# Keys and queries of a chunk by seven block products in place of eight

## The chip, the cores and the metric

The kernel runs on one core of one Trainium2 chip. The metric is the device time of one execution in microseconds (us). Smaller is better. All tensors are float32.

## The reference, cut to what matters

Two layers are computed on four images of 512 channels and 64x64 pixels. The first layer is self-attention over the 4096 pixels of an image, with 128 channels for queries, keys and values. The second layer is an involution: a 7x7 filter whose 49 weights are made for every pixel. Both add their input back.

```python
# layer 0, for each of 4 images; xf has 512 channels and 4096 pixels
q = wq @ xf + bq            # 128 x 4096
k = wk @ xf + bk            # 128 x 4096
v = wv @ xf + bv            # 128 x 4096
attn = softmax(q.T @ k)     # 4096 x 4096
x = wo @ (v @ attn.T) + bo + x
# layer 1
o = relu(s1 * (W1 @ x) + b1)                   # 128 channels
w = Ws @ relu(sr * (Wr @ o) + br) + bs         # 49 weights for each of 8 groups and each pixel
y = sum over the 49 taps of w[tap] * o shifted by the tap
out = s3 * (W3 @ y) + b3 + x
```

## The kernel before, in words

One image is handled after the other (variable b). A chunk is 512 pixels of an image, eight to an image (variable c). A chunk of x is a tile of 128 partitions by 4 blocks of channels by 512 pixels.

**The key stage** (keys_values) of an image goes over its chunks in the order 2, 3, 4, 5, 6, 7, 1, 0. For each chunk TensorE makes the keys pk (four products of a 128x128 weight block with 512 pixels, accumulated over the channels) and the values pv (sixteen products with 128 columns). ScalarE copies both out of PSUM and adds the key bias. Each product of float32 shows as two instructions in the profile.

**The attention stage** (attention) goes over blocks of 512 queries. At each of 32 steps a block of 128 keys is scored against the queries (pss), ScalarE takes the exponential (pt), TensorE accumulates the values (po), and VectorE sums the exponentials (pacc). The queries of a block (pq, four products with 512 columns, made by queries) are computed eight steps before the block begins. Those of chunk 0 are made in the key stage.

**The end of a block** (finish_block) divides by the sums, multiplies by wo (pwo), adds the residue, multiplies by W1 (p1), and writes the result with a border to DRAM (pix), from which windows of rows are read back (ring).

**The involution** runs beside all this. For two rows of pixels at a time TensorE makes the weights (pw), VectorE multiplies them with the ring (prod, line 427) and GpSimd adds the products up (acc, line 447). Such a multiplication with its addition is called a tap here. Then the sum is turned (turned), multiplied by W3 (py), added to x, and stored.

**What sets the order.** The program keeps an account of its own time: every matmul adds its columns times 0.43/256 us to a variable pe, and takes adds the cost of an operation to the account of VectorE or GpSimd. chores is called between matmuls; it lets the end of a block, the close of an involution unit, and the taps take a step. A tap waits while VectorE is more than 3.5 us ahead of pe in the account (4.5 in the last image) or GpSimd more than lag (4.0 in the key stage, 7.5 in attention). What is not done when attention ends is done in a tail, in which TensorE shares the additions.

**Buffers.** The exponentials lie in five tiles of the pool pt, scores in two PSUM banks (s), po and pacc in one bank each, the general products in two (mm). x has six tiles. All loads and stores of this part go through SyncE's one queue in the order of the program.

The lines that the change and the prediction touch: load_x at 215, keys_values at 589, queries at 626, attention at 779, the main loop at 837, and the wait of a tap at 392.

Of the kernel before, what the change touches and what calls it, by code (L numbers as in the profile page):

```python
# [8 lines left out]
F32 = mybir.dt.float32  # L9
# [6 lines left out]
P = 128  # L16
# [52 lines left out]

PE_COLUMN = 0.43 / 256  # L70
DVE_OP, POOL_OP = 0.7, 1.28
DVE_TAPS, POOL_TAPS = (0.16, 0.27), (0.19, 0.55)
ROW_US, X_US, PIX_US, LAND_US = 2.2, 3.8, 1.5, 3.0
HOP_US = 0.8
# [15 lines left out]
def fast_path(  # L90
# [22 lines left out]
    def pool(name, bufs, **kw):  # L113
# [37 lines left out]
    okr = const.tile([P, 1], F32, name="okr")  # L151


    turns = [
        scratch.tile([CH // P, P, P], F32, tag=f"turns{i}", name=f"turns{i}") for i in range(2)
    ]
# [14 lines left out]
    reds, sums_c = {}, {}  # L171
    written = {}
    landing = {}
    lag = 0.0
    low, load = 0, 0

    def until(us):
# [40 lines left out]
        nc.sync.dma_start(xs[b, c], x_r[b, :, :, c * CH : (c + 1) * CH])  # L218


    for cols in (slice(0, P), slice(P, O_WV)):
        nc.scalar.dma_start(wt[:, cols], wts[:, cols])
    nc.scalar.dma_start(vec, vecs)
    c0, c1 = KEYS[:2]
    xs = {(0, c0): xpool.tile([P, CT, CH], F32, tag="x", name=f"x_0_{c0}")}
    for t in range(CT):
        nc.sync.dma_start(xs[0, c0][:, t, :], x_r[0, :, t, c0 * CH : (c0 + 1) * CH])
    nc.sync.dma_start(wt[:, O_WV:O_WQ], wts[:, O_WV:O_WQ])
    load_x(0, c1)
    nc.sync.dma_start(wt[:, O_WQ:], wts[:, O_WQ:O_WR])  # L230
    nc.vector.memset(ones, 1.0)

    warm = ps.tile([P, P], F32, tag="mm", name="warm")
# [13 lines left out]
    def w_slice(off, t):  # L247
        return wt[:, off + t * P : off + (t + 1) * P]
# [4 lines left out]
    def mm(o, lhsT, rhs, start=True, stop=True, shared=1):  # L253
        pe_us(rhs.free_size() * PE_COLUMN / shared)
        return nc.tensor.matmul(o, lhsT=lhsT, rhs=rhs, start=start, stop=stop)  # L255
# [52 lines left out]
    def chores():  # L308
        step(finishing, 1)
        step(closing, 1)  # L310
        pace()
# [40 lines left out]
    def involution():  # L352
        nonlocal low, due
        while True:
# [24 lines left out]
            for o, (tiles, x, dy, n) in enumerate(ops):  # L379
                if ending:  # L380
                    sums = parts[tiles[0]]
                if o and dy >= DYS[1][0] > ops[o - 1][2]:
                    low = base + UR
                    pump()
                    if tail and units:
                        early[units[0]] = weights(*units[0])
                        copies[units[0]] = copied(*units[0], early[units[0]])
                rows = [(base + dy + t * 2) % RING for t in range(NT)]
                while base + dy + n + 2 * tiles[-1] > load:
                    yield "wait"  # L390
                landed = max(landing[base + dy + 2 * t + i] for t in tiles for i in range(n))
                while not tail and (
                    pe < max(begin, landed)
                    or free["dve"] > pe + (4.5 if b == B - 1 else 3.5)
                    or free["pool"] > pe + lag
                ):
                    yield "wait"
                first = x == 0 and dy < DYS[1][0]
                maker = adder = None
                if tail:  # L400
                    if pw_copy is None:
                        pw_copy = copies.pop((b, u), None) or copied(b, u, pw)
                    maker, adder = share(
                        n * len(tiles) * P, not first, first or ending and o >= len(ops) - 6
                    )
                cost = n * len(tiles) / NT
                free["pool"] = max(free["pool"], takes("dve", DVE_TAPS[0] + DVE_TAPS[1] * cost))
                takes("pool", POOL_TAPS[0] + POOL_TAPS[1] * cost)
                due -= cost
                d0 = dy - DYS[dy >= DYS[1][0]][0]  # L410
                prod, p0 = acc, d0
                if not first:
                    home = tailpools[1] if maker == "dve" else prods
                    prod, p0 = home.tile(
                        [P, NT, 4, P], F32, tag="prod", name=f"prod_{b}_{u}_{o}"
                    ), 0
                nt, these = len(tiles), slice(tiles[0], tiles[-1] + 1)
                col = (x * K + dy) * G
                row = rows[tiles[0]]
                lines = ring[:, row : row + n, x, :]  # L420
                image = bass.AP(
                    tensor=lines.tensor, offset=lines.offset,
                    ap=[lines.ap[0], [(rows[1] - rows[0]) * K * P, nt], [K * P, n], [1, P]],
                )
                made = prod[:, these if first else slice(0, nt), p0 : p0 + n, :]
                maps = pw_copy if maker == "pool" else pw
                product = (nc.gpsimd if maker == "pool" else nc.vector).tensor_tensor(  # L427
                    made.rearrange("p t d (g c) -> p t d g c", g=G),
                    image.rearrange("p t d (g c) -> p t d g c", g=G),
                    maps[:, these, col : col + n * G].unsqueeze(3)  # L430
                    .broadcast_to([P, nt, n * G, GC])
                    .rearrange("p t (d g) c -> p t d g c", d=n),
                    ALU.mult,
                )
                if not tail:
                    tc.keep_in_program_order(product)
                if first:
                    pass
                elif adder == "pe":

                    closes = ending and o == len(ops) - 1
                    if ending and o == len(ops) - 3:
                        drain(sums)
                        add_sums(sums["pa"], acc, False, tiles)
                    adds.append((spent[maker], o + 100 * u, sums, prod, tiles, n, closes))
                else:
                    nc.gpsimd.tensor_tensor(  # L447
                        acc[:, these, d0 : d0 + n, :], acc[:, these, d0 : d0 + n, :],
                        prod[:, :nt, :n, :], ALU.add,
                    )  # L450
                if tail:
                    drain()
                if ending and (o == len(ops) - 1 or ops[o + 1][0] != tiles):
                    closing.append(turn_last(b, u, tiles, acc, sums))
                yield
# [130 lines left out]
            nc.sync.dma_start(out_r[b, :, :, c * CH + off : c * CH + off + n], xt)  # L586


    def keys_values(b):
        kt = kvpool.tile([P, N], F32, tag="k", name=f"k_{b}")  # L590
        vT = kvpool.tile([P, N // P, P], F32, tag="v", name=f"v_{b}")

        for i, c in enumerate(KEYS):
            for k in KEYS[i + 1 : i + 3]:
                if (b, k) not in xs:
                    load_x(b, k)
            if c == 0:

                q = queries(b, 0, 0, CH)
            if b < 2 and i == 4:  # L600
                for rows in (slice(0, PAD), slice(PAD + H, None)):
                    nc.sync.dma_start(pix[b][rows].rearrange("r w c -> w r c"), zero)
                for cols in (slice(0, PAD), slice(PAD + W, None)):
                    nc.sync.dma_start(pix[b][PAD : PAD + H, cols, :], zero[:H])
            xt = xs[b, c] if c < KEEP else xs.pop((b, c))
            pk = ps_s.tile([P, CH], F32, tag="s", name=f"pk_{b}_{c}")
            for t in range(CT):
                mm(pk, w_slice(O_WK, t), xt[:, t, :], t == 0, t == CT - 1)
                if t % 2:
                    chores()  # L610
            nc.scalar.activation(
                kt[:, c * CH : (c + 1) * CH], pk, AF.Identity, bias=v1(V_BK)
            )
            pv = ps1.tile([P, 4, P], F32, tag=("po", "acc")[i % 2], name=f"pv_{b}_{c}")
            for j in range(4):
                for t in range(CT):
                    mm(
                        pv[:, j, :], xt[:, t, j * P : (j + 1) * P], w_slice(O_WV, t),
                        t == 0, t == CT - 1,
                    )  # L620
                if j % 2:
                    chores()
            nc.scalar.copy(vT[:, 4 * c : 4 * c + 4, :], pv)
        return kt, vT, q

    def queries(b, c, off, n):
        xt = xs[b, c][:, :, off : off + n]
        pq = ps.tile([P, CH], F32, tag="mm", name=f"pq_{b}_{c}_{off}")[:, :n]
        for t in range(CT):
            mm(pq, w_slice(O_WQ, t), xt[:, t, :], t == 0, t == CT - 1)  # L630
        q = work2.tile([P, CH], F32, tag="q", name=f"q_{b}_{c}_{off}")[:, :n]
        nc.scalar.activation(q, pq, AF.Identity, bias=v1(V_BQ))
        return q


# [200 lines left out]

    taps = [involution()]
    for b in range(B):
        lag = POOL_LAG[0]
        kv = keys_values(b)  # L840
        lag = POOL_LAG[1]
        if b == 0:

            pb = ps.tile([P, CT], F32, tag="mm", name="pb")
# [435 lines left out]
```

## Time and profile before

| what | value |
|---|---|
| median of 3 runs | 2587.23 us (2586.75 to 2587.34) |
| the profiled execution | 2587.14 us |
| its span in the profile | 2585.2 us, so 1.9 us lie around it |
| TensorE busy | 2570.4 us |
| VectorE busy | 1862.6 us |
| GpSimd busy | 1825.2 us |
| ScalarE busy | 838.2 us |
| granted clock of TensorE | 0.999 |
| DMA | 243 MB, 38.9% of 16 engines' span in SyncE's queue |

The profile page lists busy time by engine, the span in 40 slices, the DMA queues, and the chain of work that ended last, followed back from the last instruction. Groups of instructions can be asked for by line and shape, with the mean duration of one. Records of consecutive matmuls overlap, so the distance between starts in the chain, not the mean duration, says what a matmul costs in a row.

The key stages of the four images lie at 5 to 65, 616 to 690, 1249 to 1322 and 1878 to 1955 us, and the last score of the last image ends at about 2530 us. What follows is the tail.

### The profile page before, as it was taken

The numbers are of one execution on the slowest core, as the hardware profiler recorded it, in microseconds if no ns is written. First come the engines' busy times: TensorE is split into PE (matmuls) and PEld (weight loads), VectorE is DVE, ScalarE is ACT, GpSimd is POOL, SyncE is SP. The second block draws the span as 40 slices with busy tenths as digits, with TensorE's granted clock in tenths as the row PEclk, the third lists the DMA queues.
The fourth block names the chain that finished last, engine by engine and source line by source line (L and its number), as shares of the span: only waits on it lengthen the run. The fifth ranks groups of instructions, "written<-read, shape, count | busy, mean of one in ns | idle before, by whom it ended". The sixth has DMA issues, their size and how long they took to land.

```text
span 2585.2 us, 24342 instructions
## 1 busy us (share of the span) xinstructions
PE 2570.4 (99%) x7367; PEld 1229.3 (48%) x7367; DVE 1862.6 (72%) x2678; ACT 838.2 (32%) x1386; POOL 1825.2 (71%) x1207
## 2 busy tenths in 40 slices
PE   9999999999999999999999999999999999999998
PEld 7444444445544444444554444444465444444476
DVE  0347778887585777888667667878857678787888
ACT  1333333332233333333223333333322333333331
POOL 0006788877881778888786368888788567887887
PEclk9999999999999999999999999999999999999999
DMA  6033233445615343234661434433364431332343
GB/s 238 1 74 62 58 77 83 98 102 148 151 60 114 64 102 69 68 81 99 166 153 41 108 69 96 102 70 92 79 181 112 110 90 47 90 78 61 78 95 101
DMA packets 209049, 243.36 MB, mean 94 GB/s; under 512 B 109640, under 2 KB 129040, under 8 KB 208784
## 3 DMA queue, kind: packets, MB, share of 16 engines
q1 hardware_dynamic: 208480, 241.39, 38.9%
q8 instruction: 59, 0.97, 0.2%
q14 instruction: 78, 0.64, 0.1%
q10 hardware_dynamic: 432, 0.36, 0.1%
HBM read 192.65 MB, written 49.06 MB: 93 GB/s over the span
## 4 chain that ended last, share of the span: by engine, by line
PE 92%; POOL 4%; DVE 3%; issue 1%; ACT 0%; DVEq 0%; POOLq 0%
PE pss L255 32%; PE po L255 31%; PE pv L255 4%; PE pk L255 4%; PE pq L255 4%; PE p L255 4%; PE pwo L255 4%; PE py L255 4%; POOL acc L447 4%; PE pw L255 2%; DVE prod L427 1%; DVE pacc L828 1%; PE pr L255 1%; PE pa L259 1%; POOL acc L462 0%
## 5 line engine op out<-in xcount | busy, mean ns | idle before, releaser
L447 POOL TENSOR_TENSOR acc<-acc,prod 128x768 f32<-128x768 f32 (+3 forms) x1052 | 1682.8, 1617 | 737.9 <-DVE prod L427 694.6
L255 PE MATMUL pss<-q,k 128*128 128x512 f32 (+1 forms) x2112 | 1055.7, 584 | 0.0
L255 PE MATMUL po<-pt,v 128*128 128x512 f32 (+1 forms) x2112 | 1047.3, 580 | 0.0
L797 ACT ACTIVATE pt<-pss 128x512 f32<-128x512 f32 x1024 | 611.1, 597 | 1242.6 <-PE pss L255 1188.8
L427 DVE TENSOR_TENSOR prod<-ring,pw 128x768 f32<-128x768 f32 (+3 forms) x1086 | 874.7, 840 | 46.0 <-POOL acc L447 44.9
L828 DVE TENSOR_TENSOR pacc<-pacc,pt 128x512 f32<-128x512 f32 x958 | 664.8, 694 | 237.9 <-ACT pt L797 209.9
L255 PEld LDWEIGHTS po<-pt,v 128*128 128x128 f32 x2112 | 398.8, 190 | 480.9 <-issue 460.4
L255 PEld LDWEIGHTS pss<-q,k 128*128 128x128 f32 x2112 | 391.4, 190 | 466.8 <-issue 462.0
L508 DVE STREAM_TRANSPOSE turned<-acc 128x256 f32<-128x256 f32 x48 | 21.4, 445 | 217.9 <-POOL acc L462 217.9
L255 PE MATMUL py<-accT,wt 128*128 128x512 f32 (+1 forms) x256 | 130.1, 590 | 4.5 <-DVE x L577 4.5
L255 PE MATMUL pwo<-on,wt 128*128 128x512 f32 (+1 forms) x264 | 128.6, 580 | 0.1
L462 POOL TENSOR_TENSOR acc<-acc 128x512 f32<-128x512 f32 x122 | 121.4, 995 | 9.6
L255 PEld LDWEIGHTS pv<-wt,x 128*128 128x128 f32 x1024 | 119.6, 192 | 15.3 <-issue 15.1
L577 DVE SCALAR_TENSOR_TENSOR x<-py,vec,x 128x512 f32<-128x512 f32 (+2 forms) x136 | 96.4, 711 | 36.2 <-PE py L255 35.7
L255 PE MATMUL pv<-wt,x 128*128 128x128 f32 x1024 | 120.2, 275 | 0.0
L255 PE MATMUL p<-x,wt 128*128 128x512 f32 (+1 forms) x264 | 119.3, 580 | 0.0
L255 PE MATMUL pk<-x,wt 128*128 128x512 f32 x256 | 117.1, 596 | 0.0
L706 ACT ACTIVATE x<-x,vec 128x512 f32<-128x512 f32 (+1 forms) x132 | 92.9, 706 | 74.2 <-PE p L255 58.1
L255 PE MATMUL pq<-x,wt 128*128 128x512 f32 (+1 forms) x264 | 115.3, 579 | 0.0
L679 DVE SCALAR_TENSOR_TENSOR x<-pwo,bo,x 128x512 f32<-128x512 f32 (+1 forms) x132 | 95.1, 727 | 21.3 <-PE pwo L255 19.9
L427 DVE TENSOR_TENSOR acc<-ring,pw 128x1024 f32<-128x1024 f32 (+1 forms) x85 | 78.7, 945 | 15.6 <-PE pw L255 15.6
L255 PEld LDWEIGHTS pq<-x,wt 128*128 128x128 f32 x264 | 50.1, 190 | 59.7 <-issue 56.4
(74 smaller groups left out, 727.0 us busy)
## 6 DMA issues: line engine op xcount, KB each, us to landing
x<-x_dram SPq DMA_DIRECT2D x55, 1024.0 KB, 5.7
ring<-pix SPq DMA_DIRECT2D x74, 448.0 KB, 7.0
ring<-pix SPq DMA_DIRECT2D x24, 1344.0 KB, 9.7
out_dram<-x SPq DMA_DIRECT2D x31, 1024.0 KB, 4.5
ring<-pix SPq DMA_DIRECT2D x24, 896.0 KB, 10.5
ring<-pix SPq DMA_DIRECT2D x30, 672.0 KB, 10.9
ring<-pix SPq DMA_DIRECT2D x6, 2240.0 KB, 19.5
pix<-o1t SPq DMA_DIRECT2D x192, 32.0 KB, 1.7
```

The lines of the kernel that those rows point to most:

```text
L255: return nc.tensor.matmul(o, lhsT=lhsT, rhs=rhs, start=start, stop=stop)
L259: nc.tensor.matmul(o, lhsT=lhsT, rhs=ident, start=start, stop=stop, is_transpose=True)
L427: product = (nc.gpsimd if maker == "pool" else nc.vector).tensor_tensor(made.rearrange("p t d (g c) -> p t d g c", g=G), image.rearrange(" ...
L447: nc.gpsimd.tensor_tensor(acc[:, these, d0 : d0 + n, :], acc[:, these, d0 : d0 + n, :], prod[:, :nt, :n, :], ALU.add,)
L462: nc.gpsimd.tensor_tensor(acc[:, :, :n, :], acc[:, :, :n, :], acc[:, :, n : 2 * n, :], ALU.add)
L508: nc.vector.transpose(blocks.rearrange("p (t k q) -> p t k q", t=NT, q=TB), acc[:, :, 0, :].rearrange("p t (k q) -> p t k q", q=TB),)
L577: nc.vector.scalar_tensor_tensor(xt[:, t, :], py, v1(V_S3 + t), xt[:, t, :], ALU.mult, ALU.add)
L679: nc.vector.scalar_tensor_tensor(xt[:, t, :], pw, bo[:, t : t + 1], xt[:, t, :], ALU.add, ALU.add)
L706: nc.scalar.activation(xt[:, t, :], xt[:, t, :], AF.Identity, bias=v1(V_B3 + t))
L797: nc.scalar.activation(pt, pss, AF.Exp)
L828: nc.vector.tensor_tensor(paccs[k], paccs[k], pt, ALU.add)
```

## The change

The weights of keys and queries are stacked to 256 rows by 512 channels, and cut into two by two blocks; a chunk of x is cut into two by two blocks of 256 channels by 256 pixels. Their product is formed by Strassen's scheme in Winograd's form: seven products of blocks (m1 to m7) in place of eight, each of two matmuls with 256 columns. So a chunk's keys and queries are made together in the key stage.

- Sums of the weights (s1, s2, s4, and a difference put in place of the first half of wq) are made once, by VectorE, in the first chunk.
- Four differences of blocks of x (pixel_sums, 128x512 each) are made per chunk: for an image's first chunk two on VectorE and two on GpSimd, else all four on GpSimd, one chunk ahead, in tiles of the pool pt.
- ScalarE copies m1; VectorE makes seven additions of 128x256 from PSUM, four of them with a bias.
- Queries of chunks 1 to 7 are written to DRAM (q_out) and read back by queries, where before they were computed. Queries of chunk 0 stay in SBUF.
- The values of a chunk are split: twelve of sixteen matmuls after the fourth product, the last four after the seventh. Their PSUM tile is always po; before it alternated with acc, which now holds m5 and m3. m1 and m2 share a bank of s, m6 and m7 the other.
- In the key stage a tap waits while VectorE is 2.5 us ahead (before 3.5 or 4.5) or GpSimd 2.5 (before 4.0).
- At the start the weights of values are loaded first, those of keys and queries next, the others later.

```diff
+HALF_OP = 0.4
+KEY_LAG = 2.5
...
-                    or free["dve"] > pe + (4.5 if b == B - 1 else 3.5)
+                    or free["dve"] > pe + (2.5 if making else 4.5 if b == B - 1 else 3.5)
...
+    def pixel_sums(b, c, ahead):
+        (b11, b12), (b21, b22) = halves(b, c)
+        out = []
+        for n, (x0, x1) in enumerate(((b12, b11), (b22, 0), (b22, b12), (b21, 1))):
+            pt = ptpool.tile([P, CH], F32, tag="pt", name=f"sum_{b}_{c}_{n}")
+            pt = pt.rearrange("p (t n) -> p t n", t=2)
+            slow = ahead or n > 1
+            takes("pool" if slow else "dve", POOL_OP if slow else DVE_OP)
+            (nc.gpsimd if slow else nc.vector).tensor_tensor(
+                pt, x0, out[x1] if x1 in (0, 1) else x1, ALU.subtract
+            )
+            out.append(pt)
+        return out
...
+        def product(o, w, rhs):
+            for t in range(2):
+                mm(o, w[:, t * P : (t + 1) * P], rhs[:, t, :], t == 0, t == 1)
...
+                    nc.vector.tensor_tensor(s1, q10, q1, ALU.add)
+                    nc.vector.tensor_tensor(s2, s1, k0, ALU.subtract)
+                    nc.vector.tensor_tensor(s4, k1, s2, ALU.subtract)
+                    nc.vector.tensor_tensor(q10, k0, q10, ALU.subtract)
...
+            def add(o, m, with_, bias=None):
+                takes("dve", HALF_OP)
+                if bias is None:
+                    nc.vector.tensor_tensor(o, m, with_, ALU.add)
+                else:
+                    nc.vector.scalar_tensor_tensor(o, m, v1(bias), with_, ALU.add, ALU.add)
+
+            product(m1, k0, b11)
+            nc.scalar.copy(left, m1)
+            product(m6, s2, t2)
+            product(m7, q10, t3)
+            add(right, m6, left)
+            add(q[:, :HF], m7, right)
+            product(m5, s1, t1)
+            add(q[:, HF:], m5, q[:, :HF], V_BQ)
+            add(right, m5, right)
+            if i + 1 < NCH:
+                sums = pixel_sums(b, KEYS[i + 1], True)
...
+            product(m2, k1, b21)
+            add(left, m2, left, V_BK)
+            product(m6, q1, t4)
+            add(q[:, :HF], m6, q[:, :HF], V_BQ)
+            product(m3, s4, b22)
+            add(right, m3, right, V_BK)
+            if c:
+                nc.sync.dma_start(q_out[c], q)
...
     def queries(b, c, off, n):
-        xt = xs[b, c][:, :, off : off + n]
-        pq = ps.tile([P, CH], F32, tag="mm", name=f"pq_{b}_{c}_{off}")[:, :n]
-        for t in range(CT):
-            mm(pq, w_slice(O_WQ, t), xt[:, t, :], t == 0, t == CT - 1)
         q = work2.tile([P, CH], F32, tag="q", name=f"q_{b}_{c}_{off}")[:, :n]
-        nc.scalar.activation(q, pq, AF.Identity, bias=v1(V_BQ))
+        nc.sync.dma_start(q, q_out[c][:, off : off + n])
         return q
...
-        lag = POOL_LAG[0]
+        lag, making = KEY_LAG, True
         kv = keys_values(b)
-        lag = POOL_LAG[1]
+        lag, making = POOL_LAG[1], False
```

## The prediction

> **What bounds the kernel now.** I read the page's busy row and its chain of waits first.
>
> ```profile
> PE 2570.4 (99%) x7367; PEld 1229.3 (48%) x7367; DVE 1862.6 (72%) x2678; ACT 838.2 (32%) x1386; POOL 1825.2 (71%) x1207
> ...
> PE 92%; POOL 4%; DVE 3%; issue 1%; ACT 0%; DVEq 0%; POOLq 0%
> ```
>
> TensorE is busy for 99% of the span and is 92% of the chain. The rest of the chain (POOL 4%, DVE 3%) lies mostly in the tail. So a matmul column taken away is worth its time, as long as nobody makes TensorE wait. Next the busy time by stretches (columns: length, then busy us of PE, PEld, DVE, ACT, POOL, clock, DMA share, GB/s): the key stage of image 1, a stretch of image 3's attention, and the tail.
>
> ```profile
> 616.00:690.00 74.00, 74.00 (x370) 48.12 (x369) 38.10 (x45) 15.48 (x24) 59.14 (x32) 1.00 0.68 182
> 2400.00:2500.00 100.00, 100.00 (x338) 60.20 (x337) 84.08 (x121) 36.27 (x62) 89.18 (x59) 1.00 0.43 98
> 2531.00:2585.00 54.00, 44.54 (x308) 35.41 (x307) 43.49 (x81) 7.73 (x19) 40.19 (x36) 0.97 0.39 105
> ```
>
> TensorE never pauses in the stage that is changed, even where VectorE and GpSimd are busy for 84% and 89%. GpSimd already has 59 of 74 us in the key stage: this is where the new work goes. The chain in order of time (start, length) gives the price of a matmul in a row:
>
> ```profile
> 616.26 3.43 PE pk L255 x8
> ...
> 645.43 3.57 PE pv L255 x32
> ...
> 678.72 3.43 PE pq L255 x8
> ...
> 2480.36 1.73 PE pq L255 x8
> ```
>
> Eight instructions with 512 columns take 3.43 us, 0.429 each. Eight with 256 columns (the half block of image 3) take 1.73 us, 0.216 each: half the columns cost half, with a new weight block each time.
>
> **Matmuls, on the path.** Before, a chunk's keys and queries are 16 instructions x 0.429 = 6.87 us. After, 7 products x 2 matmuls x 2 instructions = 28 x 0.216 = 6.05 us. 0.82 us less for each of 32 chunks: **-26.3 us**. The values (3.57 us a chunk) are only split. Per image the key stage grows by 8 x 6.05 - 9 x 3.43 = 17.5 us, and attention loses 7 x 3.43 = 24.0 us.
>
> **Additions, VectorE.** The nearest rows by shape:
>
> ```profile
> L447 POOL TENSOR_TENSOR acc<-acc,prod 128x512 f32<-128x512 f32 x367 | 458.7, 1274 | 101.5 <-DVE prod L427 95.1 <-PE pwo L255 5.1
> L427 DVE TENSOR_TENSOR prod<-ring,pw 128x256 f32<-128x256 f32 x136 | 55.7, 410 | 8.6 <-POOL acc L447 8.6
> L679 DVE SCALAR_TENSOR_TENSOR x<-pwo,bo,x 128x256 f32<-128x256 f32 x8 | 3.6, 477 | 0.1
> ```
>
> Three additions x 0.41 + four with bias x 0.48 = 3.15 us a chunk, 101 us in all. In the key stage VectorE had 38 of 74 us; with 25 us more it has 63 of some 92. Free time hides them, if they come in time. TensorE runs m1, m6, m7, m5 until 3.46 us after the chunk's start, values until 6.14, m2, second m6, m3 until 8.7, values until 9.6. The built program's waits show that the first addition waits for m7 as well (m6 and m7 share a bank), so at 2.6. Four additions end near 4.5. The second m6 needs the first two of them at 7.0, m3 the other two at 7.9: over 3 us of slack. At the chunk's end, m1 of the next chunk needs m2's addition (7.0 + about 0.7) at 9.6 and m6 needs the second m6's (near 8.6) at 10.5. So slack is about 1.9 us, against one or two taps (0.94 to 1.21 us) that stand between. VectorE can just hold this; cover gone, TensorE waits about a tap, 1 us, a chunk.
>
> [...]
>
> **Differences of x, GpSimd.** 120 x 1.274 = 153 us; eight more on VectorE x 0.69 (the row of sums, 128x512) = 5.5 us. Per chunk 5.1 us of 9.6. The differences for a chunk are queued after m5 of the one before (3.46). The second, which m6 needs at 10.5, needs a pt tile that m5 releases: earliest 3.5 + 1.27 = 4.7. Slack is 5.7 us. The order of the built program puts none to two additions of taps between two differences, at most 1.8 + 1.8 = 3.6 us here, so TensorE should not wait. In image 0 no tap runs in the key stage at all. But GpSimd has 59 us + 38 (30 differences x 1.27) for a stage of about 92: the taps must give way. The built program shows this: image 1's attention begins at unit 12, tap 6, where it began at unit 13, tap 7. These 15 taps are done in attention, where GpSimd still has room (11% in the stretch above).
>
> [...]
>
> **An image's first chunk.** Its first two differences stand in VectorE's queue with the last attention block's sums, behind up to five taps of 0.68 us; the other two on GpSimd behind ten additions of 1.27 us. TensorE has m1 and the values (4.4 us), then pl, which needs the sums, then m6 and m7. Walking the queue from its rows, VectorE comes through between 2.6 us (nothing late) and 5.6 us (delayed by the turn of unit 10) after the last po; GpSimd's third difference between 4.1 and 6.7, needed at 5.5. So a wait of 0 to about 1.5 us; up to 5 if GpSimd uses the 7.5 us of lead that it is allowed. I take **1 us x 3 images = +3**, as before's GpSimd ended 1.8 us after attention.
>
> **Other chunks of images 1 to 3.** 24 chunks, wait 0 to 1 us each (above). I take 0.1, **+2**, nearer to the lower end since the walk left slack everywhere.
>
> **Start.** wq now is on the path: 0.25 MB behind x, wv, wk. The values' weights, in the same place of the queue, landed by 8.1 us in before (pv's load waited for them until then); 0.25 MB more at 237 GB/s is 1.1 us; two sums x 0.41, so m6 begins near 10.3, where it could at 9.1. **+1** (0 to 2).
>
> **Queries from DRAM.** 28 writes and 29 reads in SyncE's queue. A read is issued eight steps ahead, needed six steps on, 6 x 1.72 = 10.3 us; 256 KB landed in 2.8 us in the nearest row (accT). Loads, stores and ring loads stand before it in the queue, each at most some 5 us late (the longest wait of an x load for a store was 4.8). So **0**, and if a read is held more than 7 us, TensorE waits for the excess. ScalarE loses 33 bias additions of 0.69 us in attention; it isn't the bound.
>
> **Tail.** After the last sums, VectorE's tail work by its rows is 36.4 us after, 35.8 before; GpSimd's 38.6 against 35.5, as two or three more taps are left over. They share the tail: **+2** (-1 to +4).
>
> **Sum.** -26.3 + 3 + 2 + 1 + 0 + 2 = -18.3. From the profiled execution, 2587.1 (0.1 below the median): 2568.8, say **2569 us**.
>
> **Rivals.**
> 1. *Late sums, still faster.* VectorE's additions come late behind taps: 0.5 us a chunk and 3 us an image: 24 x 0.5 + 9 = 21 in place of 5 gives 2585; half of that 2577. For it: VectorE executes in order, slack is only 1.9 us. Against: VectorE is idle for 30% of the stage.
> 2. *Slower: GpSimd becomes the bound of the key stage.* 97 us of work for 92 us; if the account lets taps in too freely, m6 waits for its second difference. It decides from 24 waits of (26.3 - 1 - 2 - 3)/24 = 0.85 us on. At 1.5 us a chunk: 2569 + 24 x 1.4 = 2603. Against it: the limit of 2.5 us of lead, and the 15 taps put off.
> 3. *Queries late.* SyncE's queue is held up behind a store: 2 us for each of 28 blocks gives 2625, for a third of them 2588. The queue's longest waits in before were for work that wasn't due.
> 4. *No saving*: alternating weights make 256 columns dearer. The row 1.73 speaks against it; 2595.
>
> **Chances.** Forecast (2560 to 2575) 0.58; rival 1 0.21, of it 0.05 above 2582; rival 2 0.13; rival 3 0.06, half of it near 2588; rival 4 0.02. A measurement of this kernel tells about 0.2% (5 us) from no change. Faster by that (below 2582): 0.58 + 0.16 = 0.74, and 0.02 of mild cases of 2 and 3: 0.76. Same: 0.08. Slower: 0.16. The range: 2560 (matmuls alone, no wait) to 2585 (rival 1 in full) leaves out some 0.2.
>
> **What would show it.** Right: product groups m with 28 instructions in 6.05 us a chunk; key stages of about 9.6 us a chunk plus what is shared; PE idle in them under 1 us a chunk; no wait of pss for a DMA; a tail of 54 to 58 us. Wrong: PE or PEld idle before m, with POOL's differences (rival 2) or VectorE's additions (rival 1) as releaser, or pss waiting for q from DRAM (rival 3).

## The result and the profile after

The changed kernel takes **2598.91 us** (median of 5 runs, 2597.89 to 2599.45); the kernel before took 2587.23 beside it. The ratio is 1.0043, 95% interval 1.0030 to 1.0056: 11.7 us slower, where 2569 was forecast, 18 us faster. The profiled execution took 2598.91 us, its span is 2596.8.

The page of the changed kernel: busy time, and the chain of waits by engine.

```profile
PE 2559.5 (99%) x7763; PEld 1305.1 (50%) x7763; DVE 1965.6 (76%) x2911; ACT 807.3 (31%) x1355; POOL 1971.4 (76%) x1325
...
PE 71%; POOL 12%; DVE 10%; issue 6%; DMA 0%; ACT 0%; POOLq 0%; DVEq 0%; ACTq 0%
```

TensorE is still busy 99% of the span, but holds only 71% of the chain, where it held 92%. Busy share says nothing here; the chain does. The stage that was changed is not where it was lost. In image 0's key stage the chain reads (start, length, what):

```profile
26.32 3.46 PE m L261 x16
29.77 2.68 PE pv L261 x24
32.45 2.59 PE m L261 x12
35.05 0.89 PE pv L261 x8
```

A chunk takes 9.62 us without a gap, 6.05 of it for the seven products, as forecast. The three stretches shown of before, now (the first 74 us of image 1's key stage, which is 89 us long now; image 3's attention; the tail):

```profile
615.80:689.80 74.00, 72.27 (x419) 61.80 (x418) 41.00 (x74) 10.85 (x20) 60.98 (x46) 1.00 0.55 164
2400.00:2500.00 100.00, 100.00 (x312) 54.89 (x311) 83.17 (x117) 36.21 (x61) 85.15 (x56) 1.00 0.40 92
2538.70:2596.70 58.00, 47.59 (x328) 37.41 (x326) 46.91 (x83) 8.70 (x21) 44.90 (x39) 0.96 0.35 97
```

The key stage has 1.7 us of idle TensorE, all at its first chunk. The tail is 4.5 us longer (58.1 for 53.6). The rest shows in TensorE's waits over the whole run (what waited, for what: us in all, times, longest):

```profile
PE pl L261 <- DVE blocks L742: 12.7, 9, 1.9
PE pw L261 <- DVE prod L433: 9.5, 8, 2.0
...
PE m L261 <- POOL sum L608: 1.1, 3, 0.4
```

pl divides a finished block by the sums of its exponentials, pw makes the weights of the next involution unit. Both wait for VectorE. The waits of pw all lie in attention, and so do 7.0 us of those of pl; 4.1 of pl stand at the first chunks of images 1 to 3 and 1.6 in the tail. The new products m hardly wait for GpSimd's differences. In the kernel before, pl does not wait at all. The longest row of TensorE's waits there, and that of pw:

```profile
PE py L255 <- DVE x L577: 4.7, 5, 1.2
...
PE pw L255 <- DVE prod L427: 0.7, 3, 0.2
```

One wait of pl in image 0's attention, in order of time (start, length):

```profile
464.61 0.45 DVE L514 STREAM_TRANSPOSE turned<-acc 128x256 f32<-128x256 f32 x1 [6.52 <-POOL acc L468]
...
477.44 2.94 DVE L433 TENSOR_TENSOR prod<-ring,pw 128x1024 f32<-128x1024 f32 x3
...
478.84 1.02 PE L261 MATMUL po<-pt,v 128*128 128x512 f32 x2
...
480.30 0.68 DVE L919 TENSOR_TENSOR sums<-pacc,pt 128x512 f32<-128x512 f32 x1
481.02 0.71 DVE L742 TRANSPOSE_TENSOR_REDUCE blocks<-sums 128x16 f32<-128x512 f32 x1
...
481.78 0.40 PE L261 MATMUL pl<-blocks,quads 128*128 128x16 f32 x2 [1.92 <-DVE blocks L742]
```

TensorE is through with its queue at 479.86; VectorE has three products of taps ahead of the block's sums and delivers at 481.73. The same block in the kernel before:

```profile
456.10 0.45 DVE L508 STREAM_TRANSPOSE turned<-acc 128x256 f32<-128x256 f32 x1 [6.53 <-POOL acc L462]
...
471.83 0.68 DVE L831 TENSOR_TENSOR sums<-pacc,pt 128x512 f32<-128x512 f32 x1
472.54 0.71 DVE L654 TRANSPOSE_TENSOR_REDUCE blocks<-sums 128x16 f32<-128x512 f32 x1
...
480.17 0.29 PE L255 MATMUL pl<-blocks,quads 128*128 128x16 f32 x2
```

There the sums were ready 6.9 us ahead of pl. In both kernels VectorE stands idle for 6.5 us at turned, the transposition of a unit's sums, until GpSimd has added them up. The transposition begins 19.9 us ahead of ScalarE's first touch of the finished po in the kernel before (476.00), and 11.8 us ahead of it in the changed kernel (476.38).

A measure for all 33 blocks, taken from the trace: from ScalarE's first touch of the finished po to the end of blocks. Before, the sums are on average 0.8 us earlier than that (at most 1.6 late), in the changed kernel 1.7 us later (at most 5.8). This is called the lateness of the sums below.

Behind a wait TensorE's granted clock can be lower, too. The changed kernel around the wait of 1.96 us that ends at 755.4 (columns: length, busy us of PE, PEld, DVE, ACT, POOL, then the clock):

```profile
754.00:756.00 2.00, 0.57 (x4) 0.33 (x4) 1.90 (x4) 0.00 (x0) 2.00 (x3) 0.97 0.00 0
756.00:758.00 2.00, 2.00 (x5) 0.83 (x3) 0.00 (x0) 0.00 (x0) 2.00 (x3) 0.50 0.00 0
758.00:760.00 2.00, 2.00 (x4) 0.72 (x3) 0.00 (x0) 0.60 (x1) 1.84 (x3) 0.68 0.00 0
```

The granted clock falls to 0.50 for 3.41 us, which by these two numbers costs another 1.7 us of work. This happened three times before the tail (5.1 us), and in the kernel before it did not happen there at all.

Outside the tail TensorE is idle for 26.8 us, 21.7 more than before; with 5.1 of halved clock and 4.5 more in the tail that is 31 us of loss. From 26.3 us faster, which the matmuls alone would give, to 11.7 us slower it is 38 us; the other 7 do not show as waits. The prediction had 8 us for all of it.

### The profile page after: what moved, and what is told of

Same layout as the page of the kernel before. It is cut to its first block, busy times and chain, and to the rows that moved or that the text cites. A ratio compares the mean times of both kernels' runs of the same rounds, so it can differ in the third digit from the quotient of the medians.

```text
span 2596.8 us, 25930 instructions
## 1 busy us (share of the span) xinstructions
PE 2559.5 (99%) x7763; PEld 1305.1 (50%) x7763; DVE 1965.6 (76%) x2911; ACT 807.3 (31%) x1355; POOL 1971.4 (76%) x1325
## 4 chain that ended last, share of the span: by engine, by line
PE 71%; POOL 12%; DVE 10%; issue 6%; DMA 0%; ACT 0%; POOLq 0%; DVEq 0%; ACTq 0%
PE pss L261 24%; PE po L261 23%; POOL acc L453 11%; PE m L261 7%; DVE prod L433 4%; PE pv L261 4%; PE pwo L261 4%; PE p L261 3%; DVE pacc L916 3%; PE py L261 3%; PE pw L261 2%; POOL acc L468 1%; DVE acc L433 1%; PE pa L265 1%; DVE x L583 1%
## 5 line engine op out<-in xcount | busy, mean ns | idle before, releaser
L433 DVE TENSOR_TENSOR prod<-ring,pw 128x768 f32<-128x768 f32 (+4 forms) x1083 | 882.1, 841 | 66.1 <-POOL acc L453 65.5
L514 DVE STREAM_TRANSPOSE turned<-acc 128x256 f32<-128x256 f32 x48 | 21.4, 445 | 203.9 <-POOL acc L468 203.9
L261 PEld LDWEIGHTS pv<-wt,x 128*128 128x128 f32 x1024 | 124.9, 192 | 9.7 <-issue 6.0
L261 PE MATMUL pv<-wt,x 128*128 128x128 f32 x1024 | 126.4, 276 | 0.1
L608 POOL TENSOR_TENSOR sum<-x 128x512 f32<-128x512 f32 x60 | 76.7, 1279 | 27.5 <-PE m L261 21.6
L714 ACT COPY v<-pv 128x512 f32<-128x512 f32 x32 | 18.8, 587 | 228.3 <-PE pv L261 228.3
L608 POOL TENSOR_TENSOR sum<-x,sum 128x512 f32<-128x512 f32 x60 | 76.2, 1270 | 12.7 <-PE m L261 12.1
## 6 DMA issues: line engine op xcount, KB each, us to landing
ring<-pix SPq DMA_DIRECT2D x28, 896.0 KB, 10.5
```

Source lines behind the costliest of these rows:

```text
L514: nc.vector.transpose(blocks.rearrange("p (t k q) -> p t k q", t=NT, q=TB), acc[:, :, 0, :].rearrange("p t (k q) -> p t k q", q=TB),)
L608: (nc.gpsimd if slow else nc.vector).tensor_tensor(pt, x0, out[x1] if x1 in (0, 1) else x1, ALU.subtract)
```

## The experiments

The theories, in the words that the expectations use. **T**: GpSimd's differences push taps out of the key stage into attention (the trace has 17 in image 1's key stage, 27 before), and there VectorE and GpSimd are then late. **R1**: attention lost 24 us an image of query matmuls, and these had given VectorE time to finish; with less of TensorE's work to hide behind it is late. **R2**: VectorE's 224 additions make it late. Ratios are to the kernel before, with 95% intervals; "idle" is TensorE's, without the tail.

**1. Queries made early**, in the kernel before. They go through DRAM, and the loads of the weights stand in another order for it; nothing else is changed.

```diff
 # before; in keys_values, after the values of each chunk
+            pq = ps.tile([P, CH], F32, tag="mm", name=f"pq_{b}_{c}")
+            for t in range(CT):
+                mm(pq, w_slice(O_WQ, t), xt[:, t, :], t == 0, t == CT - 1)
+            q = work2.tile([P, CH], F32, tag="q", name=f"q_{b}_{c}")
+            nc.scalar.activation(q, pq, AF.Identity, bias=v1(V_BQ))
+            if c:
+                nc.sync.dma_start(q_out[c], q)
 # queries() reads q_out, as in the changed kernel
```

> The kernel before with one edit: the queries of all eight chunks of an image are made in the key stage by plain products (eight matmuls more in a chunk) and go through DRAM; no Strassen products, no differences of x, no additions on VectorE. TensorE's work is that of before (2587), but 24 us of it an image are moved out of attention into the key stage. Theory T (GpSimd's 120 differences, 153 us, push taps out of the key stage into attention, where GpSimd and VectorE are then late for TensorE): GpSimd has no more to do than before and gets 24 us more room in each key stage, so no loss: 2584 to 2591. Rival R1 (attention suffers because it lost the 24 us of query matmuls an image that covered the taps): the same loss as in the changed kernel, about 8 us for each image, 2600 to 2620.

Measured: 2617.82, ratio 1.0114 (1.0097 to 1.0131), 29.5 us slower. Idle 21.4 us, halved clock 6.4 us, lateness of the sums +1.0, tail 57.8. TensorE's longest waits are again for VectorE: pl 8.1 us, pwo 5.9, pw 4.8 (in the kernel before 0, 0.1 and 0.7). No difference, no addition, no Strassen product, and a loss of this size is there. Image 1's attention even has fewer taps than before (234 products on VectorE for 246), as more fit into the longer key stage. T falls as the main cause.

**2. No differences.**

```diff
-            (nc.gpsimd if slow else nc.vector).tensor_tensor(pt, x0, ..., ALU.subtract)
-            out.append(pt)
+            out.append(nothing)    # a tile of zeros
```

> The changed kernel without its differences of x: a tile of zeros is read in place of all 128 of them (four products of each chunk are then of zeros, so keys and queries are not the reference's); all matmuls and all additions stay. Theory T: GpSimd has its work of before again, taps stay in the key stage, TensorE does not wait in attention: -26.3 from the matmuls, about +2 at the start, +0 to +4 in the tail, hence 2564 to 2572. R1 (loss of matmul cover in attention): still 2590 to 2600. R2 (VectorE's 224 additions, 101 us, are what makes it late): 2590 to 2599.

Measured: 2595.21, ratio 1.0027 (1.0017 to 1.0038); 3.7 us less than the changed kernel. Idle 23.1, halved clock 9.9 us. GpSimd's 153 us are worth 4 us. With 26 taps in image 1's key stage (27 before) next to none is pushed out, and the waits stay: T is refuted once more.

**3. No additions on VectorE.**

```diff
-                nc.vector.tensor_tensor(o, m, with_, ALU.add)    # and the form with a bias
+                nc.scalar.copy(o, m)
```

> The changed kernel with its seven additions a chunk on VectorE replaced by copies of one operand on ScalarE (sums and biases of keys and queries are left out, so they are not the reference's); all matmuls and all differences stay. R2 (VectorE's additions are the load that matters): 2565 to 2578. Theory T (GpSimd's differences are): VectorE's relief does little, 2588 to 2597. R1: 2588 to 2599.

Measured: 2600.47, ratio 1.0047 (1.0030 to 1.0064): no gain. R2 is refuted; the additions were hidden, as forecast.

**4. The scheme in image 0 alone.** Images 1 to 3 run the old code.

```diff
+            if not (b == 0):
+                ...  # the old products pk, pv, and pq in queries()
+                continue
```

> The changed scheme in image 0 alone, where no taps run in the key stage, and the three other images exactly as before. From the two traces: image 0 gains 6.6 us by its matmuls, and loses 1.7 at the start and, in the changed kernel, 4.3 in its attention. Theory T: no taps are pushed out in image 0, so the loss in its attention should come only from 24 us less of cover there; if the cover does not matter, 2582 to 2584; if R1 holds for this image, 2586 to 2589. The others as before, no loss.

Measured: 2589.68, ratio 1.0008 (0.9998 to 1.0017). That is just above R1's range, and clear of the other (2582 to 2584). Image 0 has no taps in its key stage in either kernel, and yet TensorE is idle for 4.6 us in its attention, where it was 1.3 in before; the waits reach into image 1.

**5. Five product tiles for four, and its control in the kernel before (8).**

```diff
-    prods = pool("prods", 4)
+    prods = pool("prods", 5)
```

> The changed kernel with five tiles for a tap's products instead of four; nothing else. After the first four runs the leading theory is R1: TensorE is late in attention since the query matmuls (24 us an image) no longer cover VectorE there; the way it happens is that VectorE, which executes in order, waits for GpSimd to free a product tile, and the block's sums stand behind that. The changed kernel lost 16 us of TensorE's idle time in attention and 5 us of halved clock after such waits. If the product tiles are the way (R1a): most of this goes, 2580 to 2590. If VectorE or GpSimd simply lacks time in attention, whatever the tiles (R1b): 2595 to 2601. Theory T (taps pushed out of the key stage) says nothing of the tiles.

> The kernel before with five tiles for a tap's products instead of four; nothing else: the control to the run of the changed kernel with five. R1a: before has only one wait of 1.1 us an image in attention, so 2583 to 2588. If five tiles help for another reason than the waits of the changed kernel, the gain here is as large as there.

Measured: 2598.08 (1.0039, 1.0025 to 1.0054), the control 2586.24 (0.9993, 0.9983 to 1.0003). In the changed kernel VectorE's waits for a product tile fell from 65.5 to 28.4 us, and the time did not follow: R1a fails. Of the 37 us, 22 came back as VectorE's wait at the transposition (225.6 us for 203.9). VectorE isn't late because of the tiles.

**6. A shorter lead for GpSimd in the attention of images 0 to 2.**

```diff
-        lag, making = POOL_LAG[1], False
+        lag, making = 4.5 if b < B - 1 else POOL_LAG[1], False
```

> The changed kernel with GpSimd's allowed lead in attention cut from 7.5 to 4.5 us in images 0 to 2 (image 3 as it was); nothing else. R1a (VectorE waits for product tiles because GpSimd is led too far behind): fewer than four products are then pending, VectorE does not wait, TensorE's idle time in the attention of images 0 to 2 falls from 17 us to under 6, 2578 to 2590, provided the taps that are put off fit into the 60 us around an image's change in which GpSimd is idle. R1b (no time in attention at all): taps pile up, the last ones of an image come later, 2594 to 2610.

Measured: 2594.02 (1.0023, 1.0013 to 1.0033). Image 0's attention has no idle time at all, but images 1 and 2 still have 4.6 us each, and image 3 now has 10.2 us, where the changed kernel has 1.5: the taps put off were still due. R1b's mechanism, at a smaller price than it named. The lateness fell to +0.2, and the time by only 4.9 us.

**7. The key stage's smaller limits, in the kernel before.**

```diff
-POOL_LAG = 4.0, 7.5
+POOL_LAG = 2.5, 7.5
...
-                    or free["dve"] > pe + (4.5 if b == B - 1 else 3.5)
+                    or free["dve"] > pe + (2.5 if making else 4.5 if b == B - 1 else 3.5)
```

> The kernel before with nothing but the two smaller limits of the changed kernel's key stage (VectorE's and GpSimd's lead both 2.5 us there), so that taps are pushed out of the key stage into attention, while the query matmuls stay in attention and there are no differences or additions. Theory T in what is left of it (pushed taps alone cost TensorE time in attention): some 10 taps an image later, 2592 to 2600. R1 (it is the missing query matmuls): 2586 to 2590, as before.

Measured: 2592.52 (1.0019, 1.0009 to 1.0028), at the lower end of T's expectation and outside R1's. It pushed 4 taps an image into attention and cost 4.4 us. So pushed taps do cost something, here through one new wait of 1.9 us in images 1 and 2; the lateness of the sums stayed at -1.1.

**9. Cover put back.** With run 1 the decisive one: there the cover is taken out of the kernel before, here it is put back into the changed kernel.

```diff
 # changed kernel, in queries(), beside the read from DRAM
+        xt = xs[b, c][:, :, off : off + n]
+        pq = ps.tile([P, CH], F32, tag="mm", name=f"pq_{b}_{c}_{off}")[:, :n]
+        for t in range(CT):
+            mm(pq, w_slice(O_WQ, t), xt[:, t, :], t == 0, t == CT - 1)
+        nc.scalar.activation(pq, pq, AF.Identity, bias=v1(V_BQ))
```

> The changed kernel with the old query products put back into attention beside the read from DRAM: eight matmuls with 512 columns for each block (28 blocks, 96.0 us of TensorE in all) whose result nobody reads. So TensorE has 96 us more work than in the changed kernel, with all its differences, additions and limits. R1 (the query products, eight steps ahead of each block's end, gave VectorE the time to have the block's sums ready): the changed kernel's waits in attention go (19 us of idle time and some 5 of halved clock), 2598.9 + 96 - 14 to 24 = 2671 to 2681; the block's sums end on average about a microsecond before the last po again, where they end 1.7 us after it in the changed kernel. Theory T (GpSimd's and VectorE's added work): the waits stay, 2690 to 2697.

Measured: 2665.22 (1.0301, 1.0284 to 1.0318). 96.0 us of work were added (28 x 3.43) and 66.3 came: the cover is worth **29.7 us**, more than R1's range. Its page's chain, and its longest waits of TensorE:

```profile
PE 90%; POOL 4%; DMA 2%; DVE 2%; issue 1%; SPq 0%; ACT 0%; POOLq 0%; DVEq 0%; ACTq 0%
```

```profile
PE py L261 <- DVE x L583: 5.0, 5, 1.4
PE py L261 <- DMA accT<-turns: 1.9, 2, 1.4
...
PE pw L261 <- DVE prod L433: 0.7, 3, 0.2
```

The waits of pl are gone and those of pw fell from 9.5 to 0.7. Lateness of the sums -0.6, no halved clock before the tail, key stages of images 1 to 3 without idle time, tail 53.5 us as in before. All the differences, additions, limits and reads of queries from DRAM are still in. One thing changes along with the cover: the program's account of time counts the unread products too, so the taps stand at other places in the engines' queues.

2665.2 - 96.0 = 2569.2 is the predicted time, but in part by luck. The matmuls alone would give 2561. The 8 us above it were forecast for first chunks, other chunks, start and tail (3 + 2 + 1 + 2); of these run 9 has only the start (1.9 us idle). Another 3.6 us are idle time that attention has more than before. The key stages of run 9 are 66.1 us longer than before's, where 70.0 was forecast, and its attention, which has its old matmuls again, is 11.2 us longer.

**10 and 11. A better account**, in the changed kernel and, as the control, in the kernel before.

```diff
+                if not first:
+                    free["dve"] = max(free["dve"], ends.pop(0))
                 free["pool"] = max(free["pool"], takes("dve", DVE_TAPS[0] + DVE_TAPS[1] * cost))
                 takes("pool", POOL_TAPS[0] + POOL_TAPS[1] * cost)
+                if not first:
+                    ends.append(free["pool"])    # of the last four taps
```

> The changed kernel with one more rule in the planner's account of time: a tap's product on VectorE can't begin before GpSimd has freed the fourth product tile back (the account had VectorE free of that). R1 in its form that VectorE's sums are late because the account thinks VectorE ahead of where it is: taps are then held back in time and the finish of a block pauses longer, TensorE's waits in attention fall by half or more, 2582 to 2592. If the account isn't what makes them late: 2596 to 2602.

> The kernel before with the same rule in the planner's account: the control. With the query products in attention VectorE is in time already (1.1 us of waits an image), so 2585 to 2589 by either theory.

Measured: 2589.92 (1.0010, 1.0001 to 1.0020) and 2592.10 (1.0018, 1.0008 to 1.0027). The changed kernel gains 9.0 us and the kernel before loses 4.8: with cover there was nothing to plan away. Idle is 17.4 us, halved clock 3.4, but the tail grew to 64.6. The lateness is still +1.2: the time fell by 9 us and the lateness by half a microsecond.

**12. A shorter lead for VectorE in the attention of images 0 to 2.**

```diff
-                    or free["dve"] > pe + (2.5 if making else 4.5 if b == B - 1 else 3.5)
+                    or free["dve"] > pe + (4.5 if b == B - 1 else 2.5)
```

> The changed kernel with VectorE's allowed lead in the attention of images 0 to 2 cut from 3.5 to 2.5 us (that of the key stages and of image 3 as it was); nothing else. R1 (a backlog of taps on VectorE stands before the block's sums): the sums are about 1 us earlier at each block's end, the waits for them fall by some 8 to 12 us in all, 2586 to 2593, unless the taps put off collect elsewhere. Theory T: taps are only put off further, 2597 to 2604.

Measured: 2599.08 (1.0038, 1.0025 to 1.0053), no gain, and the lateness stayed at +1.7. A miss for R1 as stated: a smaller lead in the account does not bring the sums forward.

**13. Cover at the block's start.**

```diff
+            if j == 2 and k:
+                ...  # the eight matmuls pq on the current block's x, not read
```

> The changed kernel with the query products put back as cover (result not read), but two steps after a block's start instead of eight steps before its end: 96 us more of TensorE work, as in the run with cover at the old place (2665.2, so 29.7 us less than 2598.9 + 96.0). Still open is in what way the cover helps. If VectorE only needs more time in attention, wherever (Q): 2660 to 2672 again. If the place counts, since the 3.4 us must lie shortly ahead of the block's sums so that VectorE has done its taps by then (P): most of the waits stay, 2680 to 2697.

Measured: 2696.18 (1.0416, 1.0399 to 1.0434). P's time, but not shown to be P's reason:

```profile
PE pq L261 <- DVE rls L751: 17.6, 8, 2.8
PE pw L261 <- DVE prod L433: 6.7, 3, 2.3
```

The cover itself waited there: its PSUM tile was held by the chain that divides the last block. Eight waits, 17.6 us, and halved clock behind some (13.4 us before the tail). No wait of pl is left, and the lateness of the sums is -0.25; the loss has moved to other waits. Inconclusive for P against Q.

**14. Half the cover at the old place**, four matmuls for eight.

```diff
 # against run 9
-        for t in range(CT):
-            mm(pq, w_slice(O_WQ, t), xt[:, t, :], t == 0, t == CT - 1)
+        for t in range(2):
+            mm(pq, w_slice(O_WQ, t), xt[:, t, :], t == 0, t == 2 - 1)
```

> The changed kernel with half the query products as cover at the old place: four matmuls for each block, 48 us of TensorE in all, result not read. If VectorE has a fixed lack of time in each block that all of the cover was needed for, the loss falls in proportion: 2598.9 + 48.0 - 15 = 2632 (2626 to 2638). If a short pause is enough to bring the sums in time: 2617 to 2624. If only the full pause is: 2640 to 2647.

Measured: 2638.57 (1.0202, 1.0185 to 1.0219). Half the cover brings 2598.9 + 48.0 - 2638.6 = 8.3 us of 29.7, and a lateness of 0.0, between 1.7 and -0.6. Less than in proportion, and no sign that a short pause is enough.

**15 and 16. Planned around.** The account's rule in images 0 to 2 alone; and GpSimd's lead of 4.5 in image 0, the rule in images 1 and 2.

```diff
+                freed = 0.0 if first else ends.pop(0)
+                if b < B - 1:                     # in the other run: b in (1, 2)
+                    free["dve"] = max(free["dve"], freed)
...
-        lag, making = POOL_LAG[1], False
+        lag, making = POOL_LAG[1] if b else 4.5, False    # in the other run alone
```

> The changed kernel with the rule on product tiles in the planner's account for taps of images 0 to 2 alone: with the rule everywhere (2589.9) the tail was 64.6 us long instead of 58.1. If the rule is good in the middle and bad for the tail: 2582 to 2587, at or below the kernel before. If image 3 gains by it what the tail loses: 2588 to 2592.

> The changed kernel with GpSimd's lead of 4.5 us in image 0's attention and the rule on product tiles for taps of images 1 and 2, image 3 as in the changed kernel: each stretch as in the run that had it shortest (image 0 until 607.0, images 1 and 2 630.5 and 631.8 long, the rest 708.9, sum 2578). If the stretches don't depend on each other: 2577 to 2584, faster than before. If where an image's taps stand at its end shifts the waits of the next: 2585 to 2595.

Measured: 2586.98 (0.9998, 0.9989 to 1.0008) and 2592.64 (1.0020, 1.0011 to 1.0030). The first is the best version of the changed kernel: 11.9 us less, the same as before. Idle is still 17.5 us. The second shows that the stretches do depend on each other: image 0 ended at 607.1 as hoped, and image 1 was then 10.4 us longer than with the rule throughout (640.9 for 630.5).

**17 and 18. A later transposition of a unit's sums**, in the changed kernel and in the kernel before.

```diff
-        yield from until(done + 2.0)
+        yield from until(done + 8.0)
```

> The changed kernel with one number changed: the transposition of a finished unit's sums (turned) is queued on VectorE 8.0 us after the account's end of GpSimd's work, instead of 2.0. VectorE, which executes in order, stood idle at it 48 times, 203.9 us in all, for GpSimd's last sums of the unit; everything behind it came late, the block's sums too. Theory (R1 with its origin): VectorE's lateness at the ends of blocks comes from these waits, and the 3.4 us of query products a block were the time in which it caught up. Then the waits at the transposition fall to under 60 us, the block's sums come about 1 to 2 us earlier, TensorE's waits in attention fall by more than half: 2572 to 2586, below the kernel before. If the waits only move to another instruction of VectorE behind GpSimd: 2594 to 2602.

> The kernel before with the same number changed, 2.0 to 8.0: the control. It has the same idle time of VectorE at this transposition (217.9 us in 48 waits), but hides it behind the query products, and TensorE waits 1.1 us an image in attention. By the theory little is to be had: 2583 to 2588. If a late transposition helps both alike, for a reason that has nothing to do with the removed query products: lower by 10 us or more, 2570 to 2578.

Measured: 2619.69 (1.0119, 1.0104 to 1.0134) and 2603.31 (1.0058, 1.0046 to 1.0071). Both lie above every range expected. The edit missed its aim. The row of this operation in the changed kernel, and the wait in the first of these two runs:

```profile
L514 DVE STREAM_TRANSPOSE turned<-acc 128x256 f32<-128x256 f32 x48 | 21.4, 445 | 203.9 <-POOL acc L468 203.9
```

```profile
DVE turned L514 <- POOL acc L468: 199.4, 47, 7.3
```

The transposition still stood in the same place of VectorE's queue, right behind the same three pacc and ahead of the next unit's first tap, and VectorE still idled 199 us at it. What came later was only the close of the units, which moved matmuls and waits into the key stages. So whether this idle time is why VectorE has none to spare was not tried.

## Why the prediction was wrong, point by point

- **Matmuls, -26.3.** Right: 9.62 us a chunk, without gaps. The second half of that step, "attention loses 7 x 3.43 = 24.0 us", is **the step that failed**. It books the query matmuls as work on TensorE alone, and the sum has no term for taking them out of attention. They were also 3.43 us of every 70 us block in which TensorE asked nothing of VectorE. Taken out, attention gets some 18 us an image shorter, not 24.0. Counted from an image's first score to the next image's first product (or the last po), all four get 72.7 us shorter from run 9 to the changed kernel, and 73.8 from the kernel before to run 1, where 96.0 were taken out. With what the tail and the key stages lose by it, the price is 29.7 us in the changed kernel (run 9) and 29.5 in the kernel before (run 1). That the two agree so closely is in part chance: run 1 has 1.7 us of waits of its own, of first scores for the queries of chunk 0.
- **Its size in the traces.** The changed kernel's span is 2596.8, that of run 9 less the added work 2662.3 - 96.0 = 2566.3. Of the 30.5 us between, 16.3 are idle time of TensorE outside the tail (26.8 against 10.5), 5.1 halved clock, 4.5 the tail. The other 4.6 us are not seen as waits: TensorE is busy for longer with the same matmuls.
- **Differences in the key stage, additions, queries from DRAM: 0.** Right: runs 2 and 3 bring 3.7 us and nothing, no score waited for q, and a read landed in 3.0 us. Rivals 2 (GpSimd bounds the key stage), 3 and 4 did not happen. Nor did rival 1 as it was put: VectorE's results came late, but not the additions in the key stage; it was the sums of the blocks in attention.
- **"These 15 taps are done in attention, where GpSimd still has room".** True only with the cover: run 9 does 258 taps in image 1's attention, where before did 246, with 2.5 us of idle time. I read room from shares, 11% of a stretch; shares don't tell when in a block the sums are due. Pushed taps alone cost 4.4 us in run 7.
- **An image's first chunk, 1 us each.** 1.7 each; but in run 9 the key stages of images 1 to 3 have none, so most of it, too (1.4 us of pl for the block before), was the end of a late block. **Tail, +2**: +4.5, and none in run 9. **Start, +1**: 1.8 (image 0 has 80.0 us from its first product to its first score, against 60.7 + 17.5), most of it m6's wait of 1.5 us for the sums of weights.
- **Other chunks, +2.** 0 in the key stages.
- **The clock** was not in the sum at all: 5.1 us here, 9.9 in run 2.
- The forecast gave 0.16 to slower, mostly by GpSimd in the key stage. The sign came from a stage that the sum had only credited.

What stays open: why VectorE, 81% busy in image 1's attention, has no time at a block's end, whether the cover must lie ahead of the block's end (run 13 was disturbed by a wait of its own), how much of its worth is time for VectorE and how much the other places of the taps (runs 1, 9, 13 and 14 change both, and run 15 gets back 11.9 us by the places alone), and where the 4.6 us without a wait come from.

For the first question the traces hold a lead. The 204 us that VectorE idles at the transposition are no larger in the changed kernel than before (217.9), but they lie elsewhere. In 24 of the 33 blocks a transposition begins less than 60 us ahead of ScalarE's first touch of the finished po. The median of this distance is 19.7 us in the kernel before, 18.7 in run 9 and 11.8 in the changed kernel. It is under 14 us in 21 blocks of the changed kernel, and in 19 of them the sums are 2 us late or more; in 15 blocks of run 1, all of them late; in one block of run 9; and in none of the kernel before, where no block is 2 us late. So without the query products the end of a unit falls close to the end of a block. No run changed this distance alone, and it does not settle the time: run 15 has 15 such late blocks and is as fast as the kernel before.

## What to carry to other kernels

Work on the bounding engine can be cover for another engine (worth 29.7 us in run 9): before you take it away or move it to another stage, ask who catches up while it runs, and price the stage that loses it, not only the one that gains. To test it, put the work back as a product that nobody reads; what the time then fails to grow by is the worth of the cover (and of what else moves with it, as the places of the taps here). And look at the chain and at when a result is due, since busy shares of 76% and 99% said nothing of it.

## What the runs showed of the hardware

- **Half clock behind short waits.** Before the tails of the 20 traces there are 47 stretches at clock 0.50, of 3.41 or 6.83 us. In the changed kernel they begin at 482.81, 755.88 and 1895.93 us, 80 and 334 times 3.413 us apart, and the trace gives each a length of 3.413 us. In the 3.41 us ahead of such a stretch TensorE was idle for 1.3 to 3.4 us (in these three for 1.92, 1.96 and 1.74). Not every such wait is followed by one: at the same place of an image, a wait of 1.92 us that begins at 479.9 has a stretch at 0.50 behind it, and one of 1.92 us that begins at 1116.3 has none (the clock is 1.00 from 1114 to 1122). In steps of 3.413 us counted from 482.81, the first wait lies in one step, and the second with 1.4 us in one and 0.5 in the next. That this is the reason is my reading of the two waits, and no run varied it. By these lengths the same wait costs 1.9 us, or 3.6 with the 1.7 us lost at half clock.
- **VectorE's differences and sums of weights beside GpSimd.** The differences that VectorE makes in an image's first chunk:

```profile
L608 DVE TENSOR_TENSOR sum<-x 128x512 f32<-128x512 f32 x4 | 5.3, 1314 | 4.5 <-DMA x<-x_dram 4.5
L608 DVE TENSOR_TENSOR sum<-x,sum 128x512 f32<-128x512 f32 x4 | 4.2, 1039 | 1.3 <-DMA x<-x_dram 1.3
```

  In image 0 each took 0.69 us; in images 1 to 3, beside GpSimd's additions, 1.52 and 1.15. In image 0 GpSimd was idle at the first; the second began at 7.54, ahead of GpSimd's first difference at 7.58, and then it was GpSimd that took longer, 1.77 us for 1.27. The weights' sum s2 took 1.53 us beside GpSimd's second difference, the next two of its shape, beside small GpSimd instructions (128x32), 0.47. So beside GpSimd these instructions took 0.5 to 1.1 us longer apiece. At the start of image 1's key stage the two differences stand in VectorE's queue ahead of the last block's blocks and take 2.7 us for 1.4; the wait of pl there is 1.37 us. In run 9 they take as long (1.56 and 1.16), and pl does not wait. The taps' products, whose second input lies in PSUM, kept their 0.84 us (840 ns before, 841 now). That the place of the inputs makes the difference was not shown.
